# An attention-residual block: the order of every engine's steps, from ranks to a written list

## The chip, the cores and the metric

The kernel runs on one core of a Trainium2 chip. A core has five engines that run side by side and meet only through semaphores: PE (TensorE, matrix multiplies), DVE (VectorE), ACT (ScalarE), POOL (GpSimd) and SP (SyncE, which here only issues DMAs). The metric is the device time of one execution in microseconds. Three runs of the kernel before gave 146.28, 146.13 and 146.03 us; their median, 146.13 us, is the time that the prediction is about.

## The reference

The input `x` is 8 batches of 512 rows of 1024 float32 values (16.8 MB). Each batch is cut into 8 blocks of 64 rows, the blocks are summed, and a small attention over the 8 block sums gives one vector for each batch. That vector goes through `Wo`, is added to every row, the row is normalised, and the result is added to `x` again:

```python
block_repr = inputs.reshape(B, n_blocks, block_size, H).sum(axis=2)
keys = jnp.einsum('bnh,kh->bnk', block_repr, Wk)
rms = jnp.sqrt(jnp.mean(keys * keys, axis=-1, keepdims=True) + EPS)
keys = keys / rms * rms_weight
scores = jnp.einsum('bnh,h->bn', keys, query_vectors[layer_idx])
attn = jax.nn.softmax(scores, axis=-1)
attended = jnp.einsum('bn,bnh->bh', attn, block_repr)        # one vector a batch
proj = jnp.einsum('bsh,kh->bsk', broadcast(attended), Wo)
y = inputs + proj
out = (y - mean(y)) / jnp.sqrt(var(y) + EPS) * ln_gamma + ln_beta
return inputs + out
```

Both weights are 1024 x 1024 float32 (4 MB each). Everything is float32.

## The kernel before

**Tiles.** `x` is cut into 4 groups (G0 to G3) of two batches. A group is 8 "rows"; a row `k` (0 to 31 over the whole input) is a block of 128 partitions by 1024 values, and two rows make one tile of 1 MB, which one DMA loads and another stores. There are 13 such tile buffers (`XBUFS`, L35). They hold the 8 pieces of the weights first, and the later tiles of `x` take the buffers that the weights and the stored tiles give back. So the last three loads of G3 can start only when a store has landed.

**Steps of a group (the attention, `attend`, L549).** PE sums the blocks of each tile (`sums`, L566); DVE transposes the sums (`blkT`, L579); PE multiplies by the transposed `Wk` (`keys`, four parts, L434); ACT and DVE reduce the keys (`sq` L598, `dot` L602); PE spreads the reductions (`pc`, L611 and L614); ACT, DVE, ACT and DVE make the softmax in turn (`ln` L618, `score` L625 to L631, `exp` L635, `share` L640 and L643); ACT makes the weights (`w` L649, `pick` L653). PE multiplies the block sums by the transposed `Wo` (`values`, four parts, L434) and ACT copies the result (`val`, L674). PE spreads the vector over all partitions into PSUM (`spread`, tile `pb`, L680) and makes a small table (`ptab` L687, copied by ACT as `tab` L692). For G0 the same is done in quarters as the weights arrive (L459, L481, L523). Before that, PE transposes the 16 half-pieces of the weights (`pt`, L401), and ACT or DVE copies each to SBUF (L408); `EV_DVE` (L47) names the ones that DVE copies.

**Steps of a row (`define_unit`, L718).** DVE adds the vector (`y`, L733), with the row's sum beside it; ACT squares (`sq`, L741). For a unit of two or four rows POOL makes the factors (`scale`: L786 and L787; `stat`: L791, and L796 where DVE multiplies), PE transposes them (`pl`, L801), and ACT or DVE copies them (`lt`, L808; `LT_ACT`, L38, names the units for which ACT does it). ACT makes the row's multiplier (`A`, L835), POOL multiplies (`v`, L840). For the six rows 4, 5, 19, 26, 28 and 31 PE makes the multiplier in PSUM (`pA`, L825 or L846) and DVE multiplies (`vd`, L852). PE makes the addend (`b`, L869), DVE adds it (`out`, L882), SP stores the tile (L889, and the last two tiles row by row, L895).

**Buffers between the steps.** There is one PSUM place `s1` (sums, keys, pc), one `s2` (values, ptab, pl), one `pb`, and one pair `b0`, `b1` for `b` (a row's `b` waits for the `out` that read its half). There are three buffers for `A` (L36), two for `lt`, and one for `stat` (L37): the `stat` of a unit waits for the `pl` of the unit before it.

**What sets the order.** A step is added to a `Plan` with its engine, an assumed cost, the steps that it needs and a rank (L70). `Plan.order` (L75) plays the list through with those costs and picks by start and rank; `Plan.emit` (L120) then writes the instructions in order of the planned start. On the chip each engine takes its instructions in that order, whatever is ready behind the one that waits. Where the plan leaves PE a gap, `emit` puts in multiplications whose result is not used (`e_fill`, L922): 12 fills of two instructions, 24 in all, at two places in G3. The constants `R` (L40) are the ranks, `LOADS` (L46) the order of the first 12 loads, `UNITS` (L51) the rows of each unit: 15 units, the third of four rows (4 to 7).

Of the kernel before, what the change touches and what calls it, by code (L numbers as in the profile page):

```python
# [34 lines left out]
XBUFS = 13  # L35
ABUFS = 3  # L36
STATS = 1  # L37
LT_ACT = (2, 3, 4, 5, 6, 8, 9, 10, 11, 13, 14)  # L38

R = dict(  # L40
    att1=-5.0, y=203.0, sq=32.5, A=36.0, v=65.5, out=21.0, vd=98.0, scale=-20.0, lt=-150.0,
    pl=-10.0, b=-5.0, tab0=-150.0, pA=10.0, att=10.0, hold=5.0, frac=0.2,
)
ON_DVE = (4, 19, 26, 28, 31)
ON_BOTH = (2,)
LOADS = "kxxxxkkkoooo"  # L46
EV_DVE = (7, 13, 15)  # L47
Y_PARTS = ()
EARLY_SUMS = 2
ROW_STORES = 2  # L50
UNITS = (2, 2, 4, 2, 2, 2, 2, 2, 2, 2, 2, 2, 2, 2, 2)  # L51


class Plan:
# [63 lines left out]
        return max(done), start, done  # L118

    def emit(self):  # L120
        self.end, start, done = self.order()
        self.start, self.done = dict(enumerate(start)), dict(enumerate(done))
        at = None
        for i in sorted(range(len(start)), key=lambda i: (start[i], i)):
            if self.steps[i][0] == "PE" and self.filler:

                if at is not None:
                    for _ in range(int((start[i] - at - self.SLACK) / self.FILL)):
                        self.filler[1]()
                if at is not None or i == self.filler[0]:  # L130
                    at = done[i]
            self.steps[i][2]()


# [1 line left out]
def block_attn_resid_kernel(  # L136
# [16 lines left out]
    RT = 2  # L153
# [17 lines left out]
    plan = Plan(dict(s1=1, s2=1, b=1, A=ABUFS, lt=2))  # L171
# [3 lines left out]
    PE, ACT, DVE, POOL, SP = "PE", "ACT", "DVE", "POOL", "SP"  # L175
# [121 lines left out]
    at = 0  # L297
# [29 lines left out]
    for i, what in enumerate(LOADS):  # L327
        at = LOADS[:i].count(what)
# [22 lines left out]
    i = plan.add(PE, 1.1, e_pqw, [there], rank=-310, takes="s2")  # L351
    i = plan.add(ACT, 0.37, lambda: nc.scalar.copy(qw, vec["q"][:, 1, :]), [i], rank=-310)
    qw_there = plan.add(DVE, 0.42, e_qw, [i], rank=-310, gives="s2")
    gam_there = []
    for half in range(2):
# [11 lines left out]
        i = plan.add(PE, 0.8, e_pgam, [there], rank=-310, takes="s2")  # L367
# [12 lines left out]
    i = plan.add(PE, 0.8, e_ptabf, [there], rank=-310, takes="s2")  # L380
# [8 lines left out]
    def transpose_w(which, s):  # L389
        out_ = []  # L390
        for h4 in range(HC // 4):
# [14 lines left out]
            def back(h4=h4, n=n, hold=hold):  # L406
                dst = (wkT, woT)[which][:, 4 * h4 : 4 * h4 + 4, s * RT * P : (s + 1) * RT * P]
                (nc.vector.tensor_copy if n in EV_DVE else nc.scalar.copy)(dst, hold["pt"])  # L408

            rank = -300 + which if which == 0 or s < NW - 1 else -330  # L410
            a = plan.add(PE, 1.0, there, [staged[which, s], bank.get(tag)], rank)
            bank[tag] = plan.add(DVE if n in EV_DVE else ACT, 1.23 if n in EV_DVE else 1.0, back, [a], rank)
            out_.append(bank[tag])
# [74 lines left out]
    def first_values(G, T, columns, share, blkT, rank):  # L488


        rank = -299.5
        T["w0"] = chain.tile([P, P], F32, tag="w", name="w0")

        def e_w0():
            nc.scalar.activation(T["w0"], weigh0, AF.Identity, scale=T["own"])

        def e_pick0():
            T["pick"] = chain.tile([P, 2, P], F32, tag="pickw", name="pickw0")
            nc.gpsimd.tensor_scalar(flat(T["pick"]), flat(pick0), T["own"], None, ALU.mult)  # L499

        def e_val0():
            T["val0"] = work.tile([P, 4, QU], F32, tag="A", name="val0")

        w0 = plan.add(ACT, 0.42, e_w0, [share], rank)
        pick_ = plan.add(POOL, 0.7, e_pick0, [share], rank)
        val0 = plan.add("join", 0.0, e_val0, [blkT], rank, takes="A")
        vals = []
        for s in range(4):
            last = plan.add(
                PE, 0.97, lambda s=s: quarter(T, "values", woT, columns, s), [blkT, *halves[1, s]], rank, takes="s2"  # L510
            )

            def e_val(s=s):
                nc.scalar.copy(T["val0"][:, s, :], T["po"])

            vals.append(plan.add(ACT, 0.37, e_val, [last, val0], rank, gives="s2"))
        spread, G["spreads"] = None, []
        for s in range(4):
            def e_spread(s=s):
                if s == 0:  # L520
                    T["pb"] = ps.tile([P, 4, QU], F32, tag="pb", name="pb0")
                    G["pb"] = flat(T["pb"])
                nc.tensor.matmul(T["pb"][:, s, :], T["w0"], T["val0"][:, s, :], start=True, stop=True)  # L523

            spread = plan.add(PE, 0.45, e_spread, [w0, vals[s], spread, *pb_free], rank)
            G["spreads"].append(spread)
        G["spread"] = spread

        def e_ptab():
            spare["s2"] = None  # L530
            T["ptab"] = ps.tile([P, 2, QU], F32, tag="s2", name="ptab0")
            for k in range(2):
                for i in range(2):
                    nc.tensor.matmul(
                        T["ptab"][:, k, :], T["pick"][:, i, :], T["val0"][:, 2 * i + k, :], start=(i == 0), stop=False
                    )
                nc.tensor.matmul(T["ptab"][:, k, :], pickv[:, k, :], gb, start=False, stop=True)

        def e_tab():
            T["tab"] = chain.tile([P, HALF], F32, tag="tab", name="tab0", bufs=2)  # L540
            nc.scalar.copy(T["tab"], flat(T["ptab"]))

        i = free["pick"] = plan.add(PE, 2.6, e_ptab, [there, pick_, *vals], R["tab0"], takes="s2")
        G["tab"] = plan.add(ACT, 0.59, e_tab, [i], rank + 0.7, gives="s2")
        for _ in range(2):
            plan.add("join", 0.0, lambda: None, [i, spread, w0, tabf_there], rank, gives="A")
        free["blkT"] = last
# [154 lines left out]
    units, where = [], {}  # L702
    for n in UNITS:
        k0 = len(where)
# [13 lines left out]
    def define_unit(u):  # L718
        nonlocal pb_free
        U = units[u]  # L720
        k0, N = U["k0"], U["n"]
# [84 lines left out]
        def e_lt():  # L806
            U["lt"] = small.tile([P, 2, P], F32, tag="lt", name=f"lt{u}")
            (nc.scalar.copy if u in LT_ACT else nc.vector.tensor_copy)(U["lt"][:, : N // RT], U["pl"][:, : N // RT])  # L808

        st_ = f"stat{g}_{u % STATS}"  # L810
        scale = plan.add(POOL, 0.6 + 0.16 * N, e_scale, squares, R["scale"])
        i = plan.add(POOL, 0.5 if any(k0 + i in ON_DVE or (k0 + i) // RT in ON_BOTH for i in range(N)) else 0.25, e_stat, [scale], R["scale"], takes=st_)
        i = plan.add(PE, 0.22 + 0.06 * N, e_pl, [i], R["pl"], takes="s2", gives=st_)
        lt = plan.add(ACT if u in LT_ACT else DVE, 0.42, e_lt, [i], R["lt"], takes="lt", gives="s2")
        for pair in range(N // RT):
            ks = [k0 + RT * pair, k0 + RT * pair + 1]
            vs = []
# [14 lines left out]
            for k in ks:  # L832
# [23 lines left out]
                elif k in ON_DVE:  # L856
                    i = plan.add(PE, 1.1, e_pA, [lt, tabf_there, *pb_free], R["pA"])
                    vs.append(plan.add(DVE, 1.14, e_vd, [i], k + R["vd"]))
                    pb_free = [vs[-1]]
                else:  # L860
                    i = plan.add(ACT, 1.05, e_A, [scale, *gam_there], k + R["A"], takes="A")
                    vs.append(plan.add(POOL, 2.36, e_v, [i], k + R["v"], gives="A"))

            def e_b(pair=pair):
# [12 lines left out]
                gives="lt" if end else None,  # L877
# [7 lines left out]
            i = plan.add("join", 0.0, lambda: None, outs, ks[0], gives="b")  # L885
# [75 lines left out]
```

## Time and profile before

| What | us |
|---|---|
| runs, median (lowest, highest) | 146.13 (146.03, 146.28) |
| the profiled execution, its own time | 148.37 |
| its span, first to last instruction | 146.7 |
| busy: PE, DVE, ACT, POOL | 126.8, 97.4, 97.5, 83.6 |
| first `y` of G0, G1, G2, G3 starts at | 45.57, 66.92, 89.76, 114.53 |
| last `out` ends at | 142.88 |

The profile is of one execution, and the times inside it are counted from its first instruction. A group of instructions is told by line, engine, operation and tile; "busy" is the time that an engine executes, and a wait is put down to the engine or DMA whose signal came last. PE's busy time is not PE at its peak, since multiplications overlap and their ends are modelled. The clock of PE is shown as a share of full speed. The four starts of a group's first `y` cut the time after the head into four stages, which are used below.

### The profile page before, as it was taken

Reading aid. Unit: us, or ns where it says so; the run is one execution under the profiler, and the core shown is the slowest. Engines: PE = TensorE matmul, PEld = TensorE weight load, DVE = VectorE, ACT = ScalarE, POOL = GpSimd, SP = SyncE. Lnnn points to the kernel's source line nnn. Section 1 sums busy time; section 2 is a strip of 40 time slices with the busy share of each in tenths; the row PEclk is TensorE's granted clock in tenths of the full one; section 3 lists DMA queues with packets and bytes.
Section 4 is the critical chain, followed back from the end, with each engine's and each line's share of the span. In section 5 each row is a group of like instructions: output and inputs, shape, how many; then the busy total and the mean of one; then the engine's idle time right before and its main releaser. Section 6 shows DMA issues by size and latency. Waiting matters only on the chain.

```text
span 146.7 us, 3132 instructions
## 1 busy us (share of the span) xinstructions
PE 126.8 (86%) x1216; PEld 70.2 (48%) x1216; DVE 97.4 (66%) x171; ACT 97.5 (66%) x165; POOL 83.6 (57%) x100
## 2 busy tenths in 40 slices
PE   0469999999999979999899989769998979999940
PEld 0434586867867525454445536214354617652300
DVE  6201010304335995777999999978898999999790
ACT  0322368457633998969976999986598989994000
POOL 7200000000200369797889899999695999999900
PEclk9999999999999999999999999987999995999555
DMA  4999999999999991339869759970607543706945
GB/s 127 436 420 416 407 404 409 410 420 414 416 418 422 420 416 76 139 154 241 331 145 315 324 210 311 380 315 18 286 0 282 223 199 159 290 36 268 404 199 237
DMA packets 7118, 42.15 MB, mean 287 GB/s; under 512 B 688, under 2 KB 704, under 8 KB 3264
## 3 DMA queue, kind: packets, MB, share of 16 engines
q1 hardware_dynamic: 7072, 41.95, 73.1%
q8 instruction: 9, 0.15, 0.4%
q14 instruction: 5, 0.04, 0.1%
q10 hardware_dynamic: 32, 0.02, 0.0%
HBM read 25.18 MB, written 16.78 MB: 286 GB/s over the span
## 4 chain that ended last, share of the span: by engine, by line
PE 50%; POOL 13%; DVE 12%; DMA 10%; issue 5%; ACT 4%; DVEq 1%; ACTq 1%; POOLq 0%; SPq 0%
PE pt L401 10%; POOL x L840 9%; DVE x L733 7%; DMA x<-in_x_dram 7%; PE b L869 6%; PE keys L434 6%; PE bs L566 4%; DMA gb<-in_L_cond_ln_beta_dram 4%; PE pA L846 4%; PE pc L926 3%; PE values L459 3%; PE keys L459 3%; PE values L434 3%; DVE x L882 2%; POOL rs L787 2%
## 5 line engine op out<-in xcount | busy, mean ns | idle before, releaser
L840 POOL TENSOR_TENSOR x<-x,A 128x1024 f32<-128x1024 f32 x26 | 61.4, 2379 | 3.1 <-ACT A L835 3.0
L733 DVE SCALAR_TENSOR_TENSOR x<-x,pb 128x1024 f32<-128x1024 f32 x32 | 37.9, 1213 | 4.6 <-PE pb L523 3.0
L882 DVE TENSOR_TENSOR x<-x,b 128x1024 f32<-128x1024 f32 x32 | 38.2, 1216 | 2.2 <-PE b L869 1.1
L741 ACT ACTIVATE sq<-x,ysum 128x1024 bf16<-128x1024 f32 x32 | 36.7, 1146 | 4.3 <-DVE x L733 3.0
L835 ACT ACTIVATE A<-gam,rs 128x1024 f32<-128x1024 f32 x26 | 29.6, 1141 | 4.0 <-POOL rs L787 3.9
L869 PE MATMUL b<-tab,lt 32*128 32x512 f32 x128 | 25.0, 696 | 0.4 <-DVE x L882 0.4
L401 PE MATMUL pt<-ident,w 128*128 128x128 f32 x128 | 17.7, 292 | 5.8 <-DMA w<-in_L_cond_Wk_dram 5.8
L401 PEld LDWEIGHTS pt<-ident,w 128*128 128x128 f32 x128 | 15.8, 196 | 9.0 <-issue 8.6
L499 POOL TENSOR_SCALAR pickw<-early,own 128x256 f32<-128x256 f32 x1 | 0.9, 941 | 32.5 <-DVE junk L643 32.5
L566 PE MATMUL bs<-x,blk 128*32 128x256 f32 x256 | 17.2, 399 | 1.9 <-DMA x<-in_x_dram 1.9
L434 PE MATMUL keys<-wkT,blkT 128*32 128x256 f32 x192 | 12.1, 400 | 1.0 <-DVE blkT L579 1.0
L566 PEld LDWEIGHTS bs<-x,blk 128*32 128x32 f32 x256 | 7.8, 113 | 10.1 <-issue 3.8
L786 POOL TENSOR_SCALAR ssq<-ssq 128x2 f32<-128x2 f32 (+1 forms) x15 | 3.4, 223 | 16.0 <-ACT sq L741 15.0
L434 PE MATMUL values<-woT,blkT 128*32 128x256 f32 x192 | 12.0, 382 | 0.0
L787 POOL TENSOR_TENSOR rs<-ssq,power 128x2 f32<-128x2 f32 (+1 forms) x15 | 11.0, 736 | 1.2
L869 PEld LDWEIGHTS b<-tab,lt 32*128 32x128 f32 x128 | 7.4, 190 | 7.8 <-DVE x L882 3.8
L408 ACT COPY wkT<-pt 128x1024 f32<-128x1024 f32 x7 | 6.8, 1016 | 5.3 <-PE pt L401 5.3
L434 PEld LDWEIGHTS keys<-wkT,blkT 128*32 128x32 f32 x192 | 5.9, 115 | 6.9 <-issue 1.7
L434 PEld LDWEIGHTS values<-woT,blkT 128*32 128x32 f32 x192 | 5.6, 109 | 6.2 <-issue 2.3
L852 DVE TENSOR_TENSOR x<-x,pA 128x1024 f32<-128x1024 f32 x6 | 7.2, 1219 | 1.2 <-PE b L869 0.8
L801 PEld LDWEIGHTS pl<-ident,stat 128*128 128x128 f32 x16 | 2.2, 145 | 12.0 <-issue 5.4
L801 PE MATMUL pl<-ident,stat 128*128 128x128 f32 x16 | 5.3, 342 | 2.2 <-POOL stat L791 1.6
(104 smaller groups left out, 141.6 us busy)
## 6 DMA issues: line engine op xcount, KB each, us to landing
x<-in_x_dram SPq DMA_DIRECT2D x16, 1024.0 KB, 13.6
out_dram<-x SPq DMA_DIRECT2D x14, 1024.0 KB, 3.9
w<-in_L_cond_Wk_dram SPq DMA_DIRECT2D x4, 1024.0 KB, 4.8
w<-in_L_cond_Wo_dram SPq DMA_DIRECT2D x4, 1024.0 KB, 19.6
out_dram<-x SPq DMA_DIRECT2D x4, 512.0 KB, 2.8
gb<-in_cond_dram ACTq DMA_DIRECT2D x1, 4.0 KB
gb<-n_L_cond_rms_weight_dram ACTq DMA_DIRECT2D x1, 4.0 KB
gb<-in_L_cond_ln_gamma_dram ACTq DMA_DIRECT2D x1, 4.0 KB
```

Of the source, the lines that this page charges most:

```text
L401: nc.tensor.transpose(pt[:, c, r * P : (r + 1) * P], stage[which, s][:, r, bass.ds(4 * h4 + c, P, step=HC)], ident)
L434: nc.tensor.matmul(hold["po"][32 * j : 32 * j + 32, :], lhs(c), wT[:, c, bass.ts(j, QU)], start=(c == 0), stop=(end and c == HC - 1),)
L459: nc.tensor.matmul(T["po"][32 * j : 32 * j + 32, :], columns(2 * j + c), wT[:, 2 * j + c, bass.ts(s, QU)], start=(c == 0), stop=(c == 1),)
L566: nc.tensor.matmul(T["bs"][32 * j : 32 * j + 32, :], blk[g], G["x"][t][:, r, bass.ts(j, QU)], start=(t == 0 and r == 0), stop=(t == G["til ...
L733: nc.vector.scalar_tensor_tensor(x_row(k), x_row(k), 1.0, G["pb"], ALU.mult, ALU.add, accum_out=U["sum"][:, i : i + 1])
L741: nc.scalar.activation(junk, x_row(k), AF.Square, bias=U["sum"][:, i : i + 1], scale=-float(H), accum_out=U["ssq"][:, i : i + 1],)
L787: nc.gpsimd.tensor_tensor(U["rs"][:, :N], ssq, power[:, :N], ALU.pow)
L801: nc.tensor.transpose(U["pl"][:, k, :], U["st"][:, RT * k : RT * k + RT].rearrange("p r i k -> p (r i k)"), ident,)
L835: nc.scalar.activation(U["A", k], gam, AF.Identity, bias=1.0, scale=U["rs"][:, k - k0 : k - k0 + 1])
L840: nc.gpsimd.tensor_tensor(x_row(k), x_row(k), U.pop(("A", k)), ALU.mult)
L869: nc.tensor.matmul(U["b", pair][r][:, i, :], U["lt"][lo : lo + 32, pair, :], G["T"]["tab"][lo : lo + 32, :], start=True, stop=True,)
L882: nc.vector.tensor_tensor(x_row(k), x_row(k), flat(U["b", pair][k % RT]), ALU.add)
```

## The change

The steps are the same. What is changed is the order in which they are written out, the size of one unit, and who does some copies:

- `emit` walks a list `ORDER` of 457 step numbers instead of the planned order; fills are named by a table, `FILLS`, one before step 343 (`b` of unit 10) and four before step 411 (`b` of unit 12): 5 fills, 10 instructions.
- `UNITS` has sixteen units of two rows. Rows 4 to 7 are units 2 and 3, and later units have a number one higher.
- `LT_ACT` holds every unit from 2 on: DVE copies `lt` twice instead of four times.
- `EV_DVE` has six of the sixteen weight copies on DVE instead of three.
- Four assumed costs change; with `ORDER` given, they set nothing.

```diff
-LT_ACT = (2, 3, 4, 5, 6, 8, 9, 10, 11, 13, 14)
+LT_ACT = (2, 3, 4, 5, 6, 7, 8, 9, 10, 11, 12, 13, 14, 15)
-EV_DVE = (7, 13, 15)
+EV_DVE = (2, 3, 6, 9, 12, 15)
-UNITS = (2, 2, 4, 2, 2, 2, 2, 2, 2, 2, 2, 2, 2, 2, 2)
+ORDER = (
+    0, 12, 1, 5, 6, 2, 3, 4, 7, 8, 9, 11, 10, 22, 24, 13, 63, 14, 25, 15, 26, 30, 27, 16, 23, 32,
...
+    437, 445, 438, 446, 449, 448, 439, 450, 442, 440, 451, 441, 452, 453, 455, 456, 454,
+)
+FILLS = {343: 1, 411: 4}
+UNITS = (2, 2, 2, 2, 2, 2, 2, 2, 2, 2, 2, 2, 2, 2, 2, 2)
     def emit(self):
-        self.end, start, done = self.order()
-        self.start, self.done = dict(enumerate(start)), dict(enumerate(done))
-        at = None
-        for i in sorted(range(len(start)), key=lambda i: (start[i], i)):
-            if self.steps[i][0] == "PE" and self.filler:
-
-                if at is not None:
-                    for _ in range(int((start[i] - at - self.SLACK) / self.FILL)):
-                        self.filler[1]()
-                if at is not None or i == self.filler[0]:
-                    at = done[i]
+        fills = FILLS
+        if ORDER:
+            sequence = ORDER
...
+        for i in sequence:
+            for _ in range(fills.get(i, 0)):
+                self.filler[1]()
             self.steps[i][2]()
```

Since the numbers can't be read, here is what the list says, engine by engine, where it differs (`W0` to `W3` and `O0` to `O3` are the pieces of `Wk` and `Wo`, `x0` to `x3` the tiles of the group named, numbers the rows):

| Engine | Before | After |
|---|---|---|
| SP, first loads | W0, x0 x1 x2 x3 of G0, W1 W2 W3, O0 O1 O2 O3 | W0, x0, W1, W2, x1 x2 x3, W3, O0 O1 O3 O2 |
| SP, last loads of G3 | load x0, store 0, load x1, store 2, load x2, store 6, store 4, store 8, load x3 | store 0, load x0, store 2, load x2, load x1, store 4, store 6, load x3, store 8 |
| PE, start | pt of W0 (first half), pqw, sums and vectors of G0, pt of W0 (second half), pt of W1 | both halves of W0, pqw, sums x0, pt of W1 and W2 between the sums and vectors |
| PE, after `values` of G1 | sums x0, sums x1 of G2, spread, pl | sums x0 of G2, spread, pl, sums x1 |
| PE, around G3 | sums x0, spread G2, ptab G2, b, sums x1, pl, sums x2, sums x3, b, pl, keys | sums x0, spread G2, sums x1, x2, x3, b, keys with one pl between; ptab G2 after keys |
| PE, last units | 6 fills before b and 6 fills before pA 26 | 1 fill before b of rows 20, 21, and 4 before b of rows 24, 25 |
| DVE, G0 | y 4, y 5, blkT, lt, y 6, lt, y 7, out 0, dot, out 1, score, out 2, share, out 3 | y 4, lt, y 5, blkT, y 6, y 7, out 1, lt, dot, out 0, score, share, out 3, out 2 |
| DVE, G2 | y 16 to 18, out 12, 13, y 19, blkT, y 20, lt, out 14, 15, y 21, dot, y 22, out 16, y 23, score, out 17, vd 19, share, out 18, 19 | y 16 to 18, blkT, y 19, out 12, 13, y 20, dot, y 21, out 15, 14, y 22, y 23, score, out 16, 17, share, vd 19, out 18, 19 |
| DVE, from y 24 | y 24, 25, out 20, 21, y 26, 27, out 22, y 28, out 23, y 29, 30, lt, out 24, y 31, out 25, vd 26 ... | y 24 to 27, out 21, 20, y 28, 29, out 23, 22, y 30, 31, out 24, 25, vd 26 ... (the rest the same) |
| POOL | per unit: scale, stat, then its v | often two scales together, v of a later row first (v 1, v 0, v 3, v 2, v 7, v 6; v 23, v 21, v 20, v 22) |
| ACT | sq in row order | sq 5, 7, 6, 4; sq 22, 23, 21; sq 25, 24; A 1, A 0, A 3, A 2; A 23, 21, 22, 20 |

## The prediction

> **What bounds the kernel now.** I read the page's shares first, then busy time by stage, then the waits of DVE, then the chain, and last the order of the instructions around each gap. The shares alone mislead: in the page's first part PE has 86% of the span and DVE 66%. By stage it turns round. The second fence cuts the trace at the first `y` of G0, G1, G2, G3 and at the last `out`; the columns are stage, length, busy us of PE, PE's weight loads, DVE, ACT, POOL, then PE's granted clock, DMA share, GB/s.
>
> ```profile
> PE 126.8 (86%) x1216; PEld 70.2 (48%) x1216; DVE 97.4 (66%) x171; ACT 97.5 (66%) x165; POOL 83.6 (57%) x100
> ```
>
> ```profile
> 45.57:66.92 21.35, 20.14 (x269) 11.20 (x268) 16.48 (x33) 18.10 (x32) 13.44 (x15) 1.00 0.65 257
> 66.92:89.76 22.84, 21.45 (x245) 10.79 (x246) 22.49 (x37) 20.09 (x37) 20.48 (x18) 1.00 0.78 266
> 89.76:114.53 24.77, 22.29 (x240) 10.02 (x241) 21.76 (x39) 20.39 (x38) 21.00 (x22) 0.93 0.55 217
> 114.53:142.88 28.35, 24.39 (x96) 11.90 (x95) 26.92 (x33) 18.42 (x29) 24.09 (x24) 0.81 0.56 227
> ```
>
> After the head DVE is the bound: 22.49 of 22.84 us in the second stage, 26.92 of 28.35 in the fourth. What an order can give back is DVE's idle time: 4.87, 0.35, 3.01 and 1.43 us. The head, up to 45.57, is PE's: from 8.98 on PE never stops. Its one free gap is before that:
>
> ```profile
> 5.77 1.94 PE L401 MATMUL pt<-ident,w 128*128 128x128 f32 x8 [5.77 <-DMA w<-in_L_cond_Wk_dram]
> 8.98 1.93 PE L342 MATMUL pqw<-gb,ident 128*32 128x256 f32 x16 [1.27 <-DMA gb<-in_L_cond_ln_beta_dram]
> ```
>
> DVE's waits in the first stage (waiting line, releaser, us, times), then the third stage's, and the chain that ended last around the third:
>
> ```profile
> DVE x L733 <- PE pb L523: 3.0, 1, 3.0
> DVE x L733 <- PE pb L680: 1.6, 1, 1.6
> ...
> DVE blkT L579 <- PE bs L566: 0.9, 1, 0.9
> ```
>
> ```profile
> 86.54 9.89 DMA x<-in_x_dram
> 96.43 0.04 issue
> 96.47 1.07 PE bs L566 x16
> ```
>
> The last tile of G3 is issued at 86.54, behind three stores in SP's queue, and lands at 96.43. The sums of G3, its keys, softmax and values follow it, so G3's first `y` comes at 114.53. And PE runs at half clock for parts of the end (same columns):
>
> ```profile
> 122.00:124.00 2.00, 2.00 (x7) 1.55 (x6) 2.00 (x4) 2.00 (x4) 1.83 (x3) 0.50 0.21 86
> 136.00:138.00 2.00, 1.65 (x7) 0.76 (x9) 1.90 (x2) 0.27 (x1) 2.00 (x2) 0.50 1.03 422
> ```
>
> **What the skill says.** The Trainium skill, "TensorE: Matmul & The Clock Gate", Part 1, says that PE is throttled by default to half its clock, that activity releases it, and that windows of about 3.4 us decide. The trace agrees: the half-clock stretches start at about 97.8 (after the wait for the tile), 121.7 and 135.3. The first two last about 3.4 us, the third to the end. The same page's table of specifications says that ScalarE, VectorE and GpSimd are strict FIFO; the trace agrees: DVE's `out` of row 1 (POOL was done with it at 58.5) started at 59.03, after a `dot` that had waited 1.27 us for ACT. "DMA: Bandwidth & Descriptors", section "Two DMAs through the same engine are not ordered", says that descriptors of one queue start in order and are pipelined, with reads and writes on separate sides; here the tile needs 9.89 us to land, where a lone first megabyte took 4.8, and the store of 89.87 is still moving.
>
> **The change, part by part.** I laid the written order out by hand, each engine in its own order, with durations of the trace start to start: `y`, `out`, `vd` 1.14; `sq` 1.15, or 1.28 before another; `A` 1.05; `v` 2.35; `scale` 1.05, `stat` 0.2 (0.4 with L796); `sums` and a part of keys or values 1.0; `b` 1.07, `pl` 0.26, `ptab` 1.95, `spread` 1.06; about 0.1 for each hop between engines.
>
> *Head.* The second half of W0 fills the gap from 7.71 to 8.98, and PE's half-clock start (pqw and the first sums took 3.6 us where 2.0 is the later rate) begins earlier, at 5.77. That would give 1.0 to 2.5. But W1 and W2 go ahead of x1, x2, x3. In the old order megabytes landed at 5.6, 8.4, 11.0, 13.4, 15.9 and so on to 35.0 for the twelfth; the k-th load lands no sooner now. So PE waits for W2 (13.4) for up to 0.8, the sums end at 22.6 instead of 18.8 and the first keys wait 0.6 for `blkT`, and O2, now last, costs 0.25 at 35.0. PE has the same other work. y 0 comes at 45.0 to 45.7; I take 45.3: **-0.3**. The six weight copies on DVE cost (1.23 - 1.01) each in latency, but DVE is idle there, and a bank has two other fillings before its next; without that cover each would be 0.2.
>
> *First stage.* Before `spread` PE now has one `sums`, not two: y 8 comes 1.0 earlier. On the way DVE still waits for the keys (0.8), `ln` (1.0) and `exp` (0.6), each with nothing movable behind it. Sum 20.2 for 21.35: **-1.15**. POOL is as far as before (v 0 to v 3 done). Unit 2 split in two costs POOL 0.6 (a scale of 1.05 and stat of 0.4 for the one of 1.27 and 0.4, plus a second stat), where it waits anyway; the extra `pl` and `lt` are 0.26 on PE and ACT.
>
> *Second stage.* DVE had almost no idle time. Now `share` of G2 ends at 41.5 after y 0, the sums of G3 need its PSUM place `s1`, and with `spread` behind them y 16 starts 43.7 after y 0: 23.5 for 22.84, **+0.65**.
>
> *Third stage.* SP issues the last load behind stores 4 and 6 only, not behind store 8, and its buffer is that of rows 4 and 5. Store 4 can go 31.0 after y 0 (at 76.3). With 5 us for it to land, and 8 to 10 for the load, the tile is there 44 to 46 after y 0; its sums stand at 45.7, that is 91.0 instead of 96.5. Keys then end 52.1 after y 0 (97.4; before about 104), softmax and values follow, `ptab` is out of the way, and DVE has work up to y 24: 8 `y`, 8 `out` and one `vd` (19.4) with `blkT`, `dot`, `score`, `share` (2.4): 21.8 for 24.77, **-2.95**. The `lt` copy moved to ACT, 0.29, is part of it.
>
> *Fourth stage.* DVE has 8 `y`, 12 `out`, 3 `vd`: 26.2, and POOL's chain v 24, 25, 27, 29, 30, each behind a scale and stat, ends together with it: 27.1 with PE at full clock. But 5 fills stand where 12 were. By my layout PE has work for about half of each 3.4 us from 66 after y 0, and from 79 on much of it uses half the array. Before, stretches with so little went to half clock (121.7, 135.3). Half clock from 79 on makes `pA` and `b` 2.1 instead of 1.05; they lie between one `out` and the next, and the last three units lose 0.8, 0.75 and 1.25: 29.9. From row 24 on throughout, POOL is caught too (`stat` waits for a late `pl`, v stands behind it): 31.6. I take 29.2 for 28.35: **+0.85**.
>
> Sum: -0.3 - 1.15 + 0.65 - 2.95 + 0.85 = -2.9. The last `out` ends at 45.3 + 20.2 + 23.5 + 21.8 + 29.2 = 140.0, and with 3.8 from there to the end (142.88 to 146.7) the span is 143.8. The profiled execution itself took 148.37, 2.24 more than the median; I carry the 2.9 over unscaled: 146.13 - 2.9 = **143.2 us**.
>
> **The rivals.** *Full clock to the end:* the fourth stage is 27.1 and the time 141.1. For it: the four fills stand just before the thin part. Against: before, 12 fills did not hold the clock at the end. *Half clock all through the fourth stage:* 31.6, time 145.6, hardly a gain. For it: the thin stretches start right at row 24. *The last tile lands as late as before* (the other side): its buffer waits for store 4, and the store of 74.17 took 10.2 us to land. At 76.3, with 10.2 and then 9.9, the tile lands at 96.4, 5.4 late for its sums at 91.0. DVE stands at `blkT` with y 19 and out 12 and 13 queued behind it, so all 5.4 go to the end: 148.6. It decides from a landing at 93.9, where the 2.9 are used up. Against: the usual store takes 3.9. *The order does nothing:* it can't, since two DVE orders differ in nearly every group; but gaps could only move, which would give 146.1.
>
> **How the numbers follow.** Forecast (142 to 144.7) 0.50; full clock 0.20 (140.5 to 142); half clock throughout, or gaps that only moved, 0.16 (144.7 to 146.4); late tile 0.14 (above 146.4). This measurement can tell about 0.2%, 0.3 us: faster is below 145.84, 0.80 from the first two and most of the third; same 0.06; slower 0.14. The range leaves out the late tile and the best of the full clock: 141.0 to 146.4.
>
> **What would show it.** Right: PE's second transposition before pqw, y 0 near 45.3; one `sums` between `values` of G1 and `spread`; no PE wait for a tile of `x` in G3, its keys over before 99; DVE over 95% busy in the third stage; half clock in the last 15 us. Wrong: a wait of `blkT` on sums above 2 us, y 0 later than 46, POOL idle before `stat` in the fourth stage by more than 2 us, or clock 1.00 to the end.

## The result, and the profile after

The changed kernel takes 143.75 us (median of 4 runs, 143.43 to 144.35) where the kernel before takes 146.19 (4 runs, 146.03 to 146.28). The ratio is 0.9839, with a 95% interval of 0.9805 to 0.9873. The prediction was 143.2 (141.0 to 146.4), faster with a chance of 0.80. One thing has to be known to read the two traces side by side: the profiled execution of the kernel before was a slow one of 148.37 us, over 1.5% above the fastest of that kernel, and that of the changed kernel an ordinary one of 144.35, so the traces differ by 4.0 us and the medians by 2.4.

The page's first part of the changed kernel, busy time and share of each engine:

```profile
PE 123.2 (86%) x1202; PEld 68.8 (48%) x1202; DVE 100.0 (70%) x172; ACT 95.2 (67%) x165; POOL 84.2 (59%) x103
```

The same trace cut at the first `y` of G0, G1, G2, G3 and at the last `out` (stage, length, busy us of PE, weight loads, DVE, ACT, POOL, PE's clock, DMA share, GB/s):

```profile
45.29:65.11 19.82, 19.51 (x252) 10.46 (x251) 16.40 (x34) 17.59 (x31) 13.71 (x15) 1.00 0.66 255
65.11:88.21 23.10, 22.67 (x263) 10.97 (x267) 22.40 (x37) 21.26 (x38) 21.85 (x22) 1.00 0.81 303
88.21:109.74 21.53, 20.45 (x238) 10.27 (x237) 21.25 (x38) 20.05 (x38) 20.37 (x20) 1.00 0.56 230
109.74:138.87 29.13, 22.86 (x84) 10.35 (x84) 26.55 (x31) 18.86 (x31) 23.64 (x24) 0.68 0.54 221
```

The stages before were 21.35, 22.84, 24.77 and 28.35. DVE's work is the same to 0.5 us in each; what went are its idle times, 1.45 us of them in the first stage and 2.7 in the third. The fourth stage is longer, and its clock is 0.68 where it was 0.81.

PE's start in the timeline, with no gap left between the first transposition and `pqw`:

```profile
5.92 3.65 PE L427 MATMUL pt<-ident,w 128*128 128x128 f32 x16 [5.92 <-DMA w<-in_L_cond_Wk_dram]
9.50 1.88 PE L368 MATMUL pqw<-gb,ident 128*32 128x256 f32 x16
```

DVE's two largest waits from 44 to 68 (waiting line, releaser, us, times, longest). The first is in the head, the second is that for the spread of G1, 1.6 before:

```profile
DVE x L759 <- PE pb L549: 2.9, 1, 2.9
DVE x L759 <- PE pb L706: 0.9, 1, 0.9
```

On PE, a wait of 0.95 for `blkT` ahead of the keys of G1 is gone (first the kernel before, then the changed one). The sums of G2 ahead of the spread start at 63.88 before and 62.95 after, which is 18.31 and 17.66 us after the first `y` of G0:

```profile
52.92 1.07 PE L434 MATMUL keys<-wkT,blkT 128*32 128x256 f32 x16 [0.95 <-DVE blkT L579]
```

```profile
53.16 2.80 PE L460 MATMUL keys<-wkT,blkT 128*32 128x256 f32 x48
```

Around the third stage the chain no longer holds a DMA. SP's queue issues the last tile of G3 at 80.78, and PE runs the sums of its last three tiles in one stretch; the bracket with a wait, 1.88 us for the tile before, is missing:

```profile
80.78 0.38 SPq L346 DMA_DIRECT2D x<-in_x_dram  x1
```

```profile
88.09 2.80 PE L592 MATMUL bs<-x,blk 128*32 128x256 f32 x48
```

Half clock came at 113.6 for 3.4 us and from about 123.8 to the end. Two windows of 2 us from that last stretch, at its start and near its end:

```profile
124.00:126.00 2.00, 2.00 (x8) 0.88 (x8) 2.00 (x3) 2.00 (x4) 1.75 (x6) 0.50 0.25 102
136.00:138.00 2.00, 0.97 (x4) 0.00 (x0) 2.00 (x3) 0.00 (x0) 0.00 (x0) 0.50 1.00 408
```

### The profile page after: what moved, and what is told of

It reads as the page before. It is cut to its first block, busy times and chain, and to the rows that moved or that the text cites. A ratio compares the mean times of both kernels' runs of the same rounds, so it can differ in the third digit from the quotient of the medians.

```text
span 142.6 us, 3107 instructions
## 1 busy us (share of the span) xinstructions
PE 123.2 (86%) x1202; PEld 68.8 (48%) x1202; DVE 100.0 (70%) x172; ACT 95.2 (67%) x165; POOL 84.2 (59%) x103
## 4 chain that ended last, share of the span: by engine, by line
PE 45%; DVE 17%; DMA 14%; POOL 7%; issue 7%; ACT 6%; DVEq 1%; ACTq 0%; POOLq 0%
DMA x<-in_x_dram 10%; DVE x L908 7%; PE pt L427 7%; DVE x L759 7%; PE b L895 7%; PE bs L592 6%; POOL x L866 5%; PE pA L872 5%; PE keys L460 4%; DMA gb<-n_L_cond_rms_weight_dram 4%; PE keys L485 3%; PE values L460 3%; PE values L485 3%; ACT sq L767 3%; PE pl L827 2%
## 5 line engine op out<-in xcount | busy, mean ns | idle before, releaser
L861 ACT ACTIVATE A<-gam,rs 128x1024 f32<-128x1024 f32 x26 | 29.0, 1143 | 0.9 <-POOL rs L813 0.9
L895 PE MATMUL b<-tab,lt 32*128 32x512 f32 x128 | 24.1, 724 | 1.8 <-DVE x L908 0.9
L427 PE MATMUL pt<-ident,w 128*128 128x128 f32 x128 | 18.4, 300 | 6.4 <-DMA w<-in_L_cond_Wk_dram 5.9
L427 PEld LDWEIGHTS pt<-ident,w 128*128 128x128 f32 x128 | 16.5, 197 | 9.4 <-issue 7.9
L592 PE MATMUL bs<-x,blk 128*32 128x256 f32 x256 | 16.4, 383 | 0.8 <-DMA x<-in_x_dram 0.5
L813 POOL TENSOR_TENSOR rs<-ssq,power 128x2 f32<-128x2 f32 x16 | 11.3, 707 | 1.3
L592 PEld LDWEIGHTS bs<-x,blk 128*32 128x32 f32 x256 | 7.2, 110 | 7.9 <-issue 2.5
L812 POOL TENSOR_SCALAR ssq<-ssq 128x2 f32<-128x2 f32 x16 | 3.6, 223 | 8.7 <-ACT sq L767 7.4
L872 PE MATMUL pA<-tabf,lt 32*128 32x512 f32 x16 | 7.2, 988 | 1.6 <-DVE x L759 0.9
L434 DVE COPY wkT<-pt 128x1024 f32<-128x1024 f32 x3 | 3.7, 1225 | 6.4 <-PE pt L427 6.4
```

Source lines behind the costliest of these rows:

```text
L427: nc.tensor.transpose(pt[:, c, r * P : (r + 1) * P], stage[which, s][:, r, bass.ds(4 * h4 + c, P, step=HC)], ident)
L592: nc.tensor.matmul(T["bs"][32 * j : 32 * j + 32, :], blk[g], G["x"][t][:, r, bass.ts(j, QU)], start=(t == 0 and r == 0), stop=(t == G["til ...
L813: nc.gpsimd.tensor_tensor(U["rs"][:, :N], ssq, power[:, :N], ALU.pow)
L861: nc.scalar.activation(U["A", k], gam, AF.Identity, bias=1.0, scale=U["rs"][:, k - k0 : k - k0 + 1])
L872: nc.tensor.matmul(U["pA", k][:, i, :], U["lt"][lo : lo + 32, pair, :], tabf[lo : lo + 32, :], start=True, stop=True,)
L895: nc.tensor.matmul(U["b", pair][r][:, i, :], U["lt"][lo : lo + 32, pair, :], G["T"]["tab"][lo : lo + 32, :], start=True, stop=True,)
```

## The experiments

This table gives, for each profiled execution, the first `y` and the stages, cut at the same five events, in us. "Clock" is PE's granted clock in the fourth stage.

| kernel | first y | 1 | 2 | 3 | 4 | clock | median |
|---|---|---|---|---|---|---|---|
| before, first profile | 45.57 | 21.35 | 22.84 | 24.77 | 28.35 | 0.81 | 146.19 |
| before, again | 45.25 | 21.35 | 22.83 | 22.38 | 27.47 | 0.91 | 145.72 |
| before, load moved | 46.56 | 21.35 | 22.84 | 21.48 | 28.02 | 0.95 | 145.34 |
| before, load and new head | 45.32 | 21.35 | 22.82 | 21.49 | 28.00 | 1.00 | 144.51 |
| before, PE kept busy at the tile | 45.20 | 21.35 | 22.84 | 22.57 | 27.52 | 0.90 | 146.17 |
| after | 45.29 | 19.82 | 23.10 | 21.53 | 29.13 | 0.68 | 143.75 |
| after, again | 45.28 | 19.82 | 23.09 | 21.54 | 28.41 | 0.82 | 143.90 |
| after, load behind store 8 | 45.18 | 19.82 | 23.10 | 27.36 | 29.12 | 0.69 | 149.86 |
| after, two sums before spread | 45.27 | 20.68 | 23.09 | 21.53 | 28.39 | 0.80 | 144.78 |
| after, old head | 46.35 | 19.90 | 23.08 | 21.53 | 29.01 | 0.78 | 144.55 |
| after, no fills | 45.20 | 19.82 | 23.08 | 21.52 | 29.50 | 0.58 | 144.54 |
| after, 20 fills | 45.26 | 19.82 | 23.10 | 21.53 | 27.13 | 1.00 | 142.67 |
| after, 20 fills, no sums before spread | 45.03 | 19.51 | 23.92 | 21.54 | 27.11 | 1.00 | 143.27 |
| after's units and costs, order by ranks | 46.13 | 21.49 | 23.60 | 23.56 | 30.12 | 0.72 | 150.24 |

The runs came in three groups, each on one chip with its own runs of the kernel before (medians 145.91, 145.67 and 145.77 us), so ratios to these are given where a difference is small.

### The kernel before, again

No edit. It asks how far the first profile stands for the kernel.

> The kernel before, unchanged, for a second profile. Its first profiled execution took 148.37 us, 2.2 more than the median of its runs; the changed kernel's took 144.35, 0.6 more than its median. Theory: the gain of 4.1 us between the two traces is partly chance of the first execution, and an execution near 146.2 shows stages (from the first y of G0, G1, G2, G3 to the last out) that are shorter by about 1.7 us in sum, mostly in the third (24.77) because its tile lands sooner. Rival: all parts of the trace are a little shorter, each stage by about 0.4 us. Ratio 1.00 in both.

145.72 us (144.41 to 147.74, 20 runs), ratio 0.9986 (0.9956 to 1.0017). Its profiled execution took 144.81, and its third and fourth stage differ from those of the first profile:

```profile
89.43:111.81 22.38, 20.70 (x240) 9.83 (x241) 21.52 (x38) 20.28 (x38) 20.98 (x22) 1.00 0.61 238
111.81:139.28 27.47, 23.38 (x96) 11.11 (x95) 27.00 (x33) 18.43 (x29) 24.10 (x24) 0.91 0.58 235
```

The tile is issued at 86.21 and lands 9.09 later, so PE waits 1.08 for it instead of 1.88, and PE's clock stays at 1.00 where the first profile had 0.93. 2.4 of the third stage's length in the first profile belonged to that execution. The four stages together are 3.3 us shorter, most of it in the third: the theory was right in kind, but had only 1.7. Against this execution the change gains 1.53 in the first stage and 0.85 in the third, loses 0.27 in the second and 1.66 in the fourth, and leaves the first `y` where it was.

### The last tile's load

The changed kernel, the load of G3's last tile (step 159) behind store 8 (step 227):

```diff
-    ..., 171, 220, 172, 223, 212, 159, 278, 225, 214, ..., 226, 227, 236, ...
+    ..., 171, 220, 172, 223, 212, 278, 225, 214, ..., 226, 227, 159, 236, ...
```

> The changed kernel with one step moved: SP issues the load of G3's last tile behind store 8, as the kernel before does, not ahead of it. Theory (the third stage owes its gain to that load): the issue moves from 80.8 to about 84.5, the tile lands at 92 to 94 instead of 88.6, the transposition of G3's sums waits for it with the y and out behind it, the third stage goes from 21.5 to 24 to 25 us, the time to 146 to 147. Rival (the slot of ptab and keys made the gain, the load was in time anyway): the tile lands before 91, third stage within 0.5 us of 21.5, time within 0.3% of 143.75.

149.86 us (149.22 to 150.34), ratio 1.027 (1.020 to 1.033). The first two stages are the same to 0.01 us, the third is 5.83 longer, where the theory had 2.5 to 3.5. The DMA is back in the chain that ended last, and the clock falls behind it (the sums take 1.93 for 16 instead of 1.07):

```profile
84.37 8.88 DMA x<-in_x_dram
93.24 0.04 issue
93.29 1.93 PE bs L592 x16
```

So one place in SP's queue is worth 3.6 us of issue time in this order, 3.4 of waiting on PE, and 6.1 on the whole kernel. That the time at half clock makes the rest of the 5.83 is likely, but no run separated it.

The other side is the kernel before with its own order and its 12 fills written down, and only that load moved ahead of store 8 (its step numbers: 158 store 4, 159 the load, 223 store 8):

```diff
+        for i in ORDER:
+            for _ in range(FILLS.get(i, 0)):
+                self.filler[1]()
+            self.steps[i][2]()
...
-    ..., 157, 158, 219, ..., 278, 222, 223, 232, 209, 240, 242, 159, 279, ...
+    ..., 157, 158, 219, ..., 278, 222, 159, 223, 232, 209, 240, 242, 279, ...
```

> The kernel before, its own order and its own fills written down step by step, with one step moved: the load of the last tile of G3 goes ahead of store 8 in SP's queue, right behind store 4. Nothing of the order of PE, DVE, ACT or POOL changes. Theory (the place of that load in SP's queue is what costs before its third stage, and its lateness is what scatters its executions from 144.4 to 148.5 us): it is issued at 82 to 84.4 instead of 86.2 to 86.5, lands before 94, PE has no wait for it, the third stage is 21.3 to 22.0 (before 22.4 in one execution and 24.8 in the other), the median 144.0 to 144.9, and all executions lie within 1.2 us. Rival (the tile's landing hardly matters, since PE reaches the sums of G3 late anyway; the gain is in the new order of PE and DVE): third stage 22.3 to 22.6, median 145.5 to 146, and the scatter stays.

145.34 us (144.44 to 146.36, 13 runs), ratio 0.998 (0.994 to 1.002). The stage did what the theory said, the time did not. These are its third and fourth stage:

```profile
90.75:112.23 21.48, 20.68 (x240) 10.04 (x241) 21.31 (x38) 19.97 (x37) 20.42 (x22) 1.00 0.53 217
112.23:140.25 28.02, 22.17 (x96) 10.71 (x96) 27.18 (x33) 18.54 (x29) 24.65 (x24) 0.95 0.56 229
```

The wait is gone and the third stage is that of the changed kernel, so the load's place accounts for all that the third stage gained. But the fourth stage is 0.55 longer than in the second profile of before: the two together are 49.50 for 49.85. It is not the clock that takes it back, for in the kernel with load and new head the fourth stage is 28.00 at full clock. POOL takes most of it back. Its last two `v` start at 132.21 in the second profile of before and at 131.92 in the kernel with load and new head, 86.96 and 86.60 us after the first `y` of G0: 0.36 earlier, where the first `y` of G3 is 0.90 earlier (65.66 for 66.56). DVE, which reaches its `out` steps sooner, waits there for POOL (0.24 at 120.48 and 0.16 at 134.32). So in the order of before an earlier third stage mostly runs into POOL's chain; no run changed that chain by itself.

### The sums ahead of spread

The changed kernel with a second `sums` of G2 (step 268) ahead of the spread of G1 (step 198):

```diff
-    ..., 195, 147, 166, 198, 144, 145, ..., 199, 268, 163, ...
+    ..., 195, 147, 166, 268, 198, 144, 145, ..., 199, 163, ...
```

> The changed kernel with one step moved: PE sums a second tile of G2 ahead of the spread of G1, as the kernel before does. Theory (the first stage's gain is this one step): the first stage is longer by 1.0 us, 20.8 for 19.8, and since DVE is busy in nearly all of the second stage all of it goes to the end: 144.7 us. Rival (y 8 is bound by ACT or DVE, or the second stage has the slack to take it): first stage longer by under 0.4, or G2's first y no later than before; time within 0.3% of 143.75.

144.78 us (144.17 to 145.47), ratio 0.995 (0.992 to 0.998). The first stage is 0.86 longer, 20.68, and no other changes but the fourth, with the clock. One `sums` is 1.0 on PE; 0.86 of it reaches the first `y` of G1.

### The fills and the clock

The changed kernel with 20 fills at eleven steps instead of 5 at two (where an expectation speaks of 19 or of 31 fills, these 20 are meant):

```diff
-FILLS = {343: 1, 411: 4}
+FILLS = {343: 2, 350: 1, 384: 2, 356: 1, 411: 6, 420: 2, 424: 1, 433: 1, 437: 2, 449: 1, 451: 1}
```

> The changed kernel with more fills in the last group: 19 instead of 5, spread over every gap of PE from row 20's b on. Theory (half clock costs the fourth stage about 2 us): the clock stays at 1.00 to about 136, the last three units lose their waits of DVE for pA and b, the fourth stage goes from 29.1 to 27.1 to 27.6, the time to 142. Rival (POOL's chain ends the kernel, or fills delay b as much as the clock would): the clock stays up but the fourth stage is over 28.6 and the time within 0.3% of 143.75 or above it. Second rival: the clock falls all the same, since half of the array's work and the fills are not enough.

142.67 us (142.63 to 143.38), ratio 0.979 (0.972 to 0.985), the fastest of all the kernels here by the medians. Its fourth stage, with the same DVE and POOL work as the changed kernel, at full clock:

```profile
109.71:136.84 27.13, 23.29 (x114) 12.05 (x114) 26.61 (x31) 18.86 (x31) 23.66 (x24) 1.00 0.57 232
```

And with none:

```diff
-FILLS = {343: 1, 411: 4}
+FILLS = {}
```

> The changed kernel without its five fills on PE; the rest as changed. Theory (PE's clock in the fourth stage is held by how much work PE has there; 31 fills held it and gave 27.1): half clock comes no later than the 123.85 of the changed kernel or in longer stretches, fourth stage 29.3 to 31.6, median 144.0 to 146. Rival (five fills hold nothing, the clock is lost by the thin stretch after 123 anyway): fourth stage 29.1, median 143.6 to 143.9.

144.54 us (144.34 to 145.0), ratio 0.994 (0.992 to 0.997).

```profile
109.62:139.12 29.50, 22.64 (x74) 9.15 (x74) 26.80 (x31) 19.05 (x31) 23.64 (x24) 0.58 0.53 218
```

The three kernels differ in their fills alone: 29.50, 29.13 and 27.13 at clocks of 0.58, 0.68 and 1.00. Half clock in the fourth stage costs 2.0 us of the changed kernel's profiled execution. That execution has the lowest clock of the nine of the changed kernel, though: over the whole span 0.922, the others 0.924 to 0.952. By the medians the 20 fills gain 1.1 us over 5 and 1.9 over none.

### The head

The changed kernel with before's order up to the spread of G0 (steps 0 to 98; the first load of G3 stays where it is) and before's choice of engines for the weight copies:

```diff
-EV_DVE = (2, 3, 6, 9, 12, 15)
+EV_DVE = (7, 13, 15)
...
-    0, 12, 1, 5, 6, 2, 3, 4, 7, 8, 9, 11, 10, 22, 24, 13, 63, ..., 97, 98, 173, ...
+    0, 12, 1, 2, 3, 4, 5, 6, 7, 8, 9, 10, 11, 54, 22, 23, 13, 63, ..., 97, 98, 173, ...
```

> The changed kernel with the head of before: its order of loads, transposes and first keys and values up to the spread of G0, and its choice of engines for the weight copies; all from the first y on is as changed. Theory (the new head moves PE's waits rather than its work: its gain of 0.3 was against one execution, and another of before had its first y at 45.25): first y at 45.2 to 45.6, the stages as in the changed kernel (19.8, 23.1, 21.5), median 143.5 to 144.1. Rival (the earlier start of PE is worth more in a typical execution): first y at 46 or later, median 144.5 or more.

144.55 us (143.84 to 145.56), ratio 0.993 (0.990 to 0.996), against 0.988 (0.983 to 0.993) for the changed kernel. The rival holds: the first `y` is at 46.35, and the time lies just above its bound. The other stages are those of the changed kernel, so 0.5% of the time is the head. The two intervals overlap, so this alone would be weak; the reverse below gives the same size.

The reverse is the kernel with before's order and the load moved, and now the head of the changed kernel as well:

```diff
-EV_DVE = (7, 13, 15)
+EV_DVE = (2, 3, 6, 9, 12, 15)
...
-    0, 12, 1, 2, 3, 4, 5, 6, 7, 8, 9, 10, 11, 54, 22, 23, 13, 63, ..., 97, 98, 99, ...
+    0, 12, 1, 5, 6, 2, 3, 4, 7, 8, 9, 11, 10, 22, 24, 13, 63, ..., 97, 98, 99, ...
```

> The kernel before with its own written order, the last load of G3 ahead of store 8, and the head of the changed kernel (order of loads, transposes, first keys and values, and the engines of the weight copies up to the first y). Everything from the first y on is before's. Theory (the old head is 0 to 1.3 longer by when PE's clock rises, since every instruction after it lies on the path to the first y; the new head waits for tiles at about 13.6 and 22 and so takes the same time in each execution): first y at 45.2 to 45.3, stages as in the kernel with the load alone (21.35, 22.84, 21.5, 27.5 to 28.4), median 144.1 to 144.8, executions within 1.2 us of each other (with the load alone they lay within 1.9). Rival (the scatter is of the end, not of the head): median 145.0 to 145.5, executions within 1.9.

144.51 us (144.19 to 145.69, 21 runs), ratio 0.993 (0.991 to 0.996). 16 of the 21 lie between 144.19 and 144.66, the other 5 between 145.46 and 145.69: wider than the theory's 1.2, but the kernel with the load alone reached 146.36. The head gives 0.8 us by the medians, 0.5% by the ratios.

The timelines tell why. With the old head everything on PE from 8.9 on is end to end, so when the clock rises shows in the first `y`. (The clock column reads 1.00 there in every trace; the rise is judged by durations, a `sums` taking 1.9 us at half clock and 1.0 at full.) First the second profile of before (first `y` 45.25), then the kernel with the load moved (46.56):

```profile
10.56 1.55 PE L566 MATMUL bs<-x,blk 128*32 128x256 f32 x16
12.03 1.13 PE L359 MATMUL pgam<-gb,ident 128*128 128x256 f32 x4
```

```profile
10.53 1.96 PE L584 MATMUL bs<-x,blk 128*32 128x256 f32 x16
12.42 2.08 PE L377 MATMUL pgam<-gb,ident 128*128 128x256 f32 x4
```

In the one, `pgam` is at its later rate (1.13); in the other it still takes 2.08. With the new head the clock's rise varies too, and comes earlier (estimates below), but PE then waits for the piece W2 or for a copy, and that takes up the difference. First the changed kernel, then the one without fills, which has the same head:

```profile
9.50 1.88 PE L368 MATMUL pqw<-gb,ident 128*32 128x256 f32 x16
13.79 0.46 PE L427 MATMUL pt<-ident,w 128*128 128x128 f32 x2 [0.47 <-ACT wkT L434]
```

```profile
9.04 1.07 PE L368 MATMUL pqw<-gb,ident 128*32 128x256 f32 x16
13.67 0.57 PE L427 MATMUL pt<-ident,w 128*128 128x128 f32 x3 [1.49 <-DMA w<-in_L_cond_Wk_dram]
```

`pqw` took 1.88 or 1.07, and the transposition after it starts within 0.12 us. In the eight profiles with the new head the first `y` lies between 45.03 and 45.32; in the five with the old one between 45.20 and 46.56, in the order in which the clock rises.

### The order by ranks

The changed kernel without its written order; units, engines and costs as changed, the fills at their two steps:

```diff
-ORDER = (0, 12, 1, ...)
+ORDER = ()
```

> The changed kernel without its written order: units of two rows, the new choice of engines for the copies and the new costs, all as changed, but ranks make the order, as in the kernel before (the fills stay at their two steps). Ranks then also place the last load ahead of store 8. Theory (the order is worth what the stages of its parts say: one sums fewer ahead of spread, about 1.0 in the first stage; the load's place comes with the units): head 45.2 to 45.6, first stage 20.9 to 21.4, third 21.3 to 22.0, median 144.2 to 145.2. Rival (the written order as a whole carries the gain, the split of the units only costs POOL 0.6): median 145.9 to 146.8.

150.24 us (149.96 to 152.87), ratio 1.029 (1.024 to 1.035): both theories missed it, the nearer by 3.4 us. Every stage is longer than in the changed kernel, by 1.67, 0.50, 2.03 and 0.99, and the first `y` is at 46.13. The load is not the reason: it is issued at 82.22, and PE never waits for it. DVE's waits from 68 to 148, in the same form as above:

```profile
DVE x L735 <- PE pb L682: 3.0, 3, 1.6
DVE x L884 <- PE b L871: 2.3, 3, 1.1
DVE x L854 <- PE pA L848: 1.2, 1, 1.2
```

The changed kernel, from 68 on, has none for `pb`, 0.8 for `b` and 1.7 for `pA`. So the changed units, engines and costs with ranks are 2.9% slower than the kernel before; it is the written order that makes them faster.

### PE's wait for the tile, filled

The kernel before, with one `sums` more in G3: the third tile is added once again with weights of zero, so that PE is busy for 1.0 us of the time that it waits for the last tile.

```diff
+                if n == 3 and t == 2:
+                    for r in range(RT):
+                        for j in range(4):
+                            nc.tensor.matmul(
+                                T["bs"][32 * j : 32 * j + 32, :], none, G["x"][t][:, r, bass.ts(j, QU)],
+                                start=False, stop=False,
+                            )
```

> The kernel before with one thing added: after the sums of the third tile of G3, PE adds the same tile again with weights of zero (one sums, 1.0 us), so that it stands idle for 0 to 0.9 instead of 1.1 to 1.9 while the last tile lands. No instruction waits longer unless the tile is there early. Theory (what makes some executions of before long is that PE's idle wait for the tile costs it the clock for 3.4 us, as from 97.8 on in its first profile, with keys of 4.39 for 3.66): third stage 22.2 to 22.7, no execution above 146.8, median 145.3 to 145.8. Rival (the tile's landing itself scatters, and the clock follows whatever PE does): executions up to 147.5 to 148.5 as in the kernel before, median 145.7 to 146.2.

146.17 us (145.1 to 147.5), ratio 1.004 (1.000 to 1.007). PE's wait is down to 0.40:

```profile
94.04 1.05 PE L575 MATMUL bs<-x,none 128*32 128x256 f32 x16
95.49 1.07 PE L568 MATMUL bs<-x,blk 128*32 128x256 f32 x16 [0.40 <-DMA x<-in_x_dram]
```

The third stage is 22.57, as the theory said, but the profiled execution is the fastest of the 13, and others are as long as 147.5. In five of the 13, 0.3 to 1.4 us of the time more than the usual 1.7 lies outside the span from first to last instruction, so part of this spread is not of any stage. That PE's idle wait, through the clock, makes the long executions of before is therefore not shown. The first profile shows the two together once (1.88 idle, then keys of 4.39 instead of 3.66); what makes such executions long stays open.

### The changed kernel again, and the last sums moved

> The changed kernel again, for more executions beside the others and beside the kernel before on one chip: first y at 45.2 to 45.3, stages 19.8, 23.1, 21.5, 28.4 to 29.2, median 143.5 to 144.4. Against the kernel before in the same call the gain is 1.5 to 2.4 us.

143.90 us (143.34 to 144.27), ratio 0.988 (0.983 to 0.993), beside 0.984 in the first comparison. The first three stages agree with those of the first profile to 0.01. The fourth is 28.41 for 29.13, with the same work: the clock stays full to 128.0, where it fell at 113.6 in the first. The expected gain of 1.5 to 2.4 us holds with 1.9.

The kernel with 20 fills, and step 267, the one `sums` of G2 still ahead of the spread of G1, behind it:

```diff
-    ..., 142, 189, 267, 195, 147, 166, 198, 144, ...
+    ..., 142, 189, 195, 147, 166, 198, 267, 144, ...
```

> The changed kernel with 31 fills (as in the run with more fills, 142.67) and the one sums of G2 that stands ahead of the spread of G1 moved behind it. Theory (DVE's last wait in the first stage, 0.93 for the spread, is the sums on PE, up to the time that the last part of the values is copied): first stage 19.4 to 19.6, median 142.2 to 142.6. Rival (the copy of the values, not the sums, ends last): first stage 19.8, median 142.6 to 142.8.

143.27 us (143.01 to 143.29), ratio 0.983 (0.979 to 0.988).

```profile
45.03:64.54 19.51, 18.76 (x240) 10.05 (x242) 16.40 (x33) 17.30 (x30) 13.45 (x14) 1.00 0.66 257
64.54:88.46 23.92, 23.20 (x279) 10.89 (x281) 22.76 (x37) 21.54 (x39) 22.00 (x24) 1.00 0.82 315
```

The first stage is 19.51, as the theory said: DVE's wait for the spread goes from 0.93 to 0.62, and the spread itself now waits 0.49 for ACT's copy of the values. But the second stage, where PE has one `sums` more, is 0.82 longer, so the median misses the theory's 142.2 to 142.6, which counted the first stage alone. The version to keep is the one with 20 fills and step 267 where it was.

## Why the prediction was right, and where its steps were not

The time lies 0.55 us above the predicted one, inside the 142 to 144.7 given to the forecast. The stages of the trace came out close to the layout by hand: 19.82, 23.10, 21.53 and 29.13 for 20.2, 23.5, 21.8 and 29.2. Its signs are there too: one `sums` between the values of G1 and the spread, no wait of PE for a tile of G3, its keys over at 96.2, DVE busy for 21.25 of 21.53 us in the third stage. The account of what gains what is less good than that looks.

- **Head, -0.3.** The first `y` is at 45.29 for 45.3. Of PE's waits, the 0.66 for `blkT` is the one named; where it has the wait for W2, this execution waits 0.47 for a copy (the kernel without fills, with the same head, waits 1.49 for W2), and the 0.48 for the tile x3 is not in it. What the step missed is that the old head has no fixed length. The prediction knew the start at half clock and that the new head begins it earlier; it read 45.57 from one execution as the length, where profiles give 45.20 to 46.56. Changed alone, in the changed kernel or in before's order, the head is worth 0.5% of the time, 0.7 to 0.8 us.
- **First stage, -1.15.** Measured -1.53. The `sums` that left the way is 0.86, not 1.0. The rest, 0.67, the prediction did not have. It lies ahead of that `sums`, which starts 0.65 earlier after the first `y` (17.66 for 18.31); PE's wait of 0.95 for `blkT`, gone after, is the likely place, which no run tried alone.
- **Second stage, +0.65.** Measured +0.26. The link from `share` to `sums` and spread is there; putting one more `sums` behind the spread made it 0.82 longer.
- **Third stage, -2.95.** The step that was mis-sized. Its mechanism is shown from both sides: with the load behind store 8 the stage is 27.36, and in the order of before, with the load alone moved, 21.48. The tile landed at about 88.6 (issued at 80.78, 7.8 to land), well before the 93.9 at which the rival of the late tile would have decided. But 24.77, from which the gain was taken, was the length of one long execution. Against the other profile of before the gain is 0.85, and with the fourth stage before gives 0.5 of it back even at full clock. The load alone gains 0.2% of the time, with an interval (0.994 to 1.002) that includes no gain.
- **Fourth stage, +0.85.** Between the first two profiles it is +0.78. The forecast was half clock from 124.3; it came at 123.8 and stayed. That it came so close is luck, for in the second profile of the same kernel it came at 128.0. Nor does the reading behind it hold, that before fell to half clock after stretches with work for about half: PE was busy for 2.57 and 3.05 of the 3.41 us ahead of its falls at 121.7 and 135.3. At full clock the stage is 27.13, where the prediction had 27.1. Against the second profile of before the loss is 1.66 (0.94 with the second profile of the changed kernel), since before keeps its clock for longer there (0.91). Both rivals of this stage can be priced: the full clock is 142.67 us for 141.1 (with 20 fills; with 5 it did not come), half clock without any fill 144.54 for 145.6.
- **The sum.** The stages and the head add to -2.9 in the prediction and to -4.0 in the two traces. The prediction carried its sum over to the median unscaled, as if the 2.24 us by which the first execution lay above the median would be there after the change too. They were not: the changed kernel's profiled execution lies 0.6 above its median. The sum was 1.1 too small and the carried excess 1.64 too large, and that the errors mostly cancel is luck. Against the second profile of before, third and fourth stage together lose 0.8 (or 0.1 with the second profile of the changed kernel), and what makes the kernel faster is the first stage (1.53, less 0.27 in the second) and the steadier head (0.7 to 0.8).

The rival that gaps only move was partly right: that is what the third and fourth stage do without the extra fills. The late tile did not come: PE waits for no tile of `x` in G3. Nor did half clock from row 24 on throughout: the clock was full up to 113.6 and from 117.0 to 123.8.

## What to carry to other kernels

Take a second profile of the kernel before, and cut both at the same events, before a stage is priced: a stage whose length differs between two executions of one kernel can't be credited with its longer value. A wait that stands in the path of every execution and takes up what varies ahead of it (here for a piece of the weights) can be worth more than one pair of profiles shows. When an order is tightened, look at what PE does in the thin last stage: there 20 fills, whose result nobody uses, held the clock and gained 1.1 us over 5, nearly half of what the whole change gained.

## What the runs showed of the hardware

- The clock's rise at the start comes between about 9 and 12 us in the eight profiles with the new head and between about 11.2 and 14.8 in the five with the old one, though PE's work begins between 5.66 and 5.98 in all of them (estimates from the durations of the transpositions, `pqw`, `sums` and `pgam`, as above). With the old head PE stands idle for 0.93 to 1.27 us of that time. The Trainium skill, "TensorE: Matmul & The Clock Gate", Part 1, says that the windows of about 3.4 us run freely and don't start with the kernel, and gives a variation of 500 ns to either side; the trace agrees with the first, but the spread of 3 us or more with either head is about a whole window.
- The same page says that the clock falls after an idle window. If idle means no work at all, the trace differs: in the changed kernel it fell at 113.6, when PE had been busy for 1.19 and 1.00 us of the two windows of 2 us from 110 to 114. In the second profile of the same kernel these 2 us windows hold the same 1.19 and 1.00, and the clock stayed. A likely reason, which no run tried, is where the windows of the clock lie: counted back from a fall in steps of 3.41 us, the window that ends at 113.59 in the first profile has PE busy for 1.61, and the one from 110.96 to 114.37 in the second for 2.19. How much work holds the clock stays open, since in the kernel before it fell after 2.57 and 3.05 of 3.41. With 20 fills the 2 us windows hold 1.62 and 2.00. First the two of the first profile, then one of the second:

```profile
110.00:112.00 2.00, 1.19 (x10) 0.31 (x8) 2.00 (x3) 2.00 (x4) 2.00 (x2) 1.00 0.80 324
112.00:114.00 2.00, 1.00 (x6) 0.56 (x3) 2.00 (x5) 2.00 (x5) 1.90 (x2) 0.90 0.51 209
```

```profile
112.00:114.00 2.00, 1.00 (x7) 0.54 (x4) 2.00 (x5) 2.00 (x5) 1.90 (x2) 1.00 0.51 209
```
